# Parameter loads move from ScalarE's queue to SP's, the first scan piece's loads to GpSimd's, and late splits wait for that piece

## The chip, the cores and the metric

The kernel runs on one core of a Trainium2 chip. The core has five engines with an instruction stream each: TensorE (PE: matrix products and transposes into PSUM), VectorE (DVE), ScalarE (ACT), GpSimd (POOL) and SyncE (SP), which here only issues transfers. ScalarE and GpSimd can issue transfers too. An engine takes its instructions in order, so one that waits holds up all behind it. The metric is the device time of one execution in microseconds (us), as the median of several runs.

## The reference

Two layers work on x of shape (8, 64, 64, 96). The first is a selective scan over images (four directions), the second a linear attention and a feed-forward layer with float quantization. The change touches only the first layer:

```python
xz = einsum('bhwc,ec->bhwe', gn(x), in_proj_w); xin, z = split(xz, 2)
xc = silu(depthwise_conv3x3(xin, conv_w) + conv_b)
xs = stack([rows of xc, columns of xc, and both reversed])      # b, K=4, 192, L=4096
dts, Bs, Cs = split(einsum('bkdl,kcd->bkcl', xs, x_proj_weight), [6, 16, 16])
delta = softplus(einsum('bkrl,kdr->bkdl', dts, dt_projs_weight) + dt_bias)
h = h * exp(delta * A) + (delta * u) * Bs                        # 16 states, step by step
y = sum over the states of (h * Cs) + D * u
x = x + out_proj(layer_norm(y) * silu(z))
```

Here `gn` is a group norm over groups of 3 channels; it needs the statistics of a whole image before the first product. The parameters that move are `conv_w`, `conv_b`, the weights of x_proj (`w_xp` in the kernel) and those of the dt projection (`dt_w`).

## The kernel before

Constants are loaded first (`scan_constants`, line 188), then three passes follow. Values that one pass hands to the next go through scratch tensors in DRAM: `u_d` (the convolved x in two orders), `z_d`, `xd_d` (the output of x_proj), `b_d` and `dt_d` (parts of xd_d split into three bfloat16 terms that add up to the float32 value), and `y_d`.

**Pass 1** (line 264) goes over the eight images in pairs. For an image, `statistics` loads eight groups of 512 tokens (tile `xs`), transposes them on TensorE and takes BN statistics on VectorE; `group_norm` turns these into a scale and a bias (`gm`), with two products with `gmat`. `projection` loads the same groups again (`xt`), transposes them, normalises them on ScalarE (`xn`), and multiplies by `w_in` and `w_mix` for x (copied into padded images, `xpad`) and z (to `z_d`). `convolution` runs nine taps of 128 x 4096 on VectorE, then ScalarE's silu into `u`, four transposed copies `ut` and the stores into `u_d`. It comes three times per pair (channels 0 to 127 of either image, and the remaining 64 of both), in the order 0, 2, 1. `x_projection` multiplies by `w_xp` in PSUM tiles `px`, copies them to `xd` (four buffers) and stores these in `xd_d`. A `split` (line 234) loads part of `xd_d` (`bq`), and alternates casts on ScalarE (`bs`) with subtractions on GpSimd, then stores into `b_d` or `dt_d`. For images 0 to 4 the splits run in pass 1; those of images 5 to 7 ("late", since `LATE` is 5), 18 in number, run in pass 2.

**Pass 2** (line 530) goes over 192 pieces of 1024 positions: pair, channel group, direction, part of the image. `prepare` loads `xdt` (6 transfers), `xb` (2) and `u` (1), makes `bT` and `delta` from them with products on TensorE and ScalarE's softplus, then `du` = delta times u on GpSimd. For each of the 16 states ScalarE computes the decay `da`, TensorE the input term in a PSUM tile `wide`, VectorE the scan `h`; `load_c` loads the rows of C broadcast over the partitions (`c`, 1 MB for two states, six buffers), GpSimd multiplies h by c, and TensorE sums over the states. Pass 3 is not touched.

What sets the order: pass 1 and pass 2 are written as generators that `yield` the engine and an estimated cost before each step, or a key that must be done first. `weave` (line 142) runs them by list scheduling when the program is built, and `InOrder` fixes the resulting order on each engine; every operation issued that way has line 91 in the profile. Unless a step is `yield`ed to `weave`, its cost is not in that schedule. In pass 1 and 2 all loads and stores are issued by SP, with two exceptions on ScalarE: the constants of `scan_constants` (`dt_w`, 36 copies from the scratch tensor `w_d`, line 219), and the parameters of pass 1. Of the latter, `later_loads` (line 296) issues `conv_w`, `conv_b` and `w_xp`, 24 transfers, and is called once before `weave` (line 524). So all of these stand ahead of ScalarE's first computation in pass 1. In the built program the transfers of SP and ScalarE signal eight completion counters in turn, and a transfer waits until the one before it on its counter has landed.

Of the kernel before, what the change touches and what calls it, by code (L numbers as in the profile page):

```python
# [42 lines left out]
P = 128  # L43
NB, HH, WW, C = 8, 64, 64, 96
L = HH * WW
DI, N, R, K = 192, 16, 6, 4
# [9 lines left out]
NS = 3  # L56
# [19 lines left out]
def load_by_type(queue, dst, src):  # L76

    queue.dma_start(dst[:, 0], src[0:P])
    queue.dma_start(dst[0:64, 1], src[P:DI])
    queue.dma_start(dst[64:P, 1], src[P:DI])  # L80
# [19 lines left out]
@with_exitstack  # L100
def vss_attn_ffn_kernel(ctx: ExitStack, tc: tile.TileContext, g: dict, out: bass.AP):
    nc = tc.nc
    consts = ctx.enter_context(tc.tile_pool(name="consts", bufs=1))
    dram = ctx.enter_context(tc.tile_pool(name="scratch", bufs=1, space=DRAM))

    ident = consts.tile([P, P], F32, name="ident")
    make_identity(nc, ident)
    mhalf = consts.tile([P, NBLK], F32, name="mhalf")
    nc.vector.memset(mhalf, -0.5)


    u_d = [[dram.tile([DI, L], F32, name=f"u_d{b}_{o}") for o in range(2)] for b in range(NB)]

    y_d = [[dram.tile([L, DI], F32, name=f"y_d{b}_{o}") for o in range(2)] for b in range(NB)]
    z_d = [dram.tile([DI, L], F32, name=f"z_d{b}") for b in range(NB)]
    xd_d = [[dram.tile([2 * NXD, L], F32, name=f"xd_d{b}_{o}") for o in range(2)] for b in range(NB)]

    b_d = [[dram.tile([2, NS, N, L], BF16, name=f"b_d{b}_{o}") for o in range(2)] for b in range(NB)]
    dt_d = [[dram.tile([2, NS, R, L], BF16, name=f"dt_d{b}_{o}") for o in range(2)] for b in range(NB)]

    engines = [InOrder(tc, e) for e in (nc.tensor, nc.vector, nc.scalar, nc.gpsimd)]
    fixed = scan_constants(tc, g, consts, dram, ident)
    pass1(tc, g, consts, ident, mhalf, engines, u_d, z_d, xd_d, b_d, dt_d)
    pass2(tc, g, ident, engines, fixed, u_d, xd_d, b_d, dt_d, y_d)
    pass3(tc, g, ident, mhalf, engines, y_d, z_d, out)

# [61 lines left out]
def scan_constants(tc, g, consts, dram, ident):  # L188

    nc = tc.nc  # L190
    KB = 2 * NS * N
    with tc.tile_pool(name="p0", bufs=1) as tmp:
        a_neg = consts.tile([P, 2, K, N], F32, name="a_neg")
        load_by_type(nc.scalar, a_neg, g["A_logs"].rearrange("(k d) n -> d k n", k=K))
        nc.scalar.activation(a_neg, a_neg, AF.Exp)
        nc.vector.tensor_scalar(a_neg, a_neg, -1.0, None, ALU.mult)
        ds_ = tmp.tile([P, 2, K], F32, name="ds_")
        load_by_type(nc.scalar, ds_, g["DsT"])
        dsum = consts.tile([P, 2], F32, name="dsum")
        nc.vector.tensor_reduce(dsum, ds_, mybir.AxisListType.X, ALU.add)  # L200
        dt_b = consts.tile([P, 2, K], F32, name="dt_b")
        load_by_type(nc.scalar, dt_b, g["dt_biasT"])

        raw = tmp.tile([R, K, DI], F32, name="raw")
        nc.scalar.dma_start(raw, g["dt_wT"])
        by_part = tmp.tile([R, NS, K, DI], BF16, name="by_part")
        for s in range(NS):
            nc.vector.tensor_copy(by_part[:, s], raw)
            if s < NS - 1:
                nc.vector.tensor_sub(raw, raw, by_part[:, s])  # L210
        w_d = dram.tile([R, NS, K, DI], BF16, name="w_d")
        nc.scalar.dma_start(w_d, by_part)
        dt_w = consts.tile([2 * NS * NS * R, 3, K, P], BF16, name="dt_w")
        nc.vector.memset(dt_w, 0.0)
        for c, j, to, ch in ((0, 0, 0, slice(0, P)), (1, 1, 0, slice(0, P)), (2, 0, 0, slice(P, DI)), (2, 1, 64, slice(P, DI))):
            for m in range(NS):
                for s in range(NS):
                    row = ((j * NS + m) * NS + s) * R
                    nc.scalar.dma_start(dt_w[row : row + R, c, :, to : to + ch.stop - ch.start], w_d[:, m, :, ch])

        sel_f = tmp.tile([KB, 2, N], F32, name="sel_f")
        of_part = ident[0:KB, 0:KB].rearrange("p (j s n) -> p j n s", j=2, n=N)
        nc.vector.tensor_reduce(sel_f, of_part, mybir.AxisListType.X, ALU.add)
        sel = consts.tile([KB, 2, N], BF16, name="sel")
        nc.vector.tensor_copy(sel, sel_f)
        sel2 = consts.tile([KB, N, P], BF16, name="sel2")
        for j in range(2):
            nc.vector.tensor_copy(sel2[:, :, 64 * j : 64 * j + 64], sel[:, j, :].unsqueeze(2).to_broadcast([KB, N, 64]))  # L230
    return a_neg, dsum, dt_b, dt_w, sel, sel2


def split(engines, pool_of, cost, src, row, rows, pieces, at, dst):

    act, pool, sp = engines
    wide, used = GRP, rows * pieces
    yield "sp", 0.7, 4.0
    bq = pool_of.tile([P, wide], F32, name="bq")
    src = src[row : row + rows].rearrange("r (s t) -> (r s) t", s=pieces)  # L240
    sp.dma_start(bq[0:used], src[:, at : at + wide])
    yield "act", 0.6
    bs = pool_of.tile([P, NS, wide], BF16, name="bs")
    act.copy(bs[0:used, 0, :], bq[0:used])
    yield "pool", cost
    pool.tensor_sub(bq[0:used], bq[0:used], bs[0:used, 0, :])
    yield "act", 0.6
    act.copy(bs[0:used, 1, :], bq[0:used])
    yield "pool", cost
    pool.tensor_sub(bs[0:used, 2, :], bq[0:used], bs[0:used, 1, :])  # L250
    yield "sp", 0.9
    half = used // 2
    for k2 in range(2):
        to = dst[k2].rearrange("e n (s t) -> (n s) e t", s=pieces)[:, :, at : at + wide]
        sp.dma_start(to, bs[half * k2 : half * (k2 + 1)])
# [5 lines left out]


@with_exitstack
def pass1(ctx, tc, g, consts, ident, mhalf, engines, u_d, z_d, xd_d, b_d, dt_d):
    nc = tc.nc
    pe, dve, act, pool = engines
    sp = InOrder(tc, nc.sync)
# [22 lines left out]
    conv_w = wp.tile([P, 2, 9], F32, name="conv_w")  # L290
    conv_b = wp.tile([P, 2, 1], F32, name="conv_b")

    w_xp = wp.tile([P, 3, 2, P], F32, name="w_xp")
    pool.memset(w_xp, 0.0)

    def later_loads():
        load_by_type(act, conv_w, g["conv_w"])
        load_by_type(act, conv_b, g["conv_b"])
        w0 = 0
        for rows in (slice(R, R + N), slice(R + N, NXD), slice(0, R)):  # L300
            wide = rows.stop - rows.start
            for k2 in range(2):
                src = slice(k2 * NXD + rows.start, k2 * NXD + rows.stop)
                act.dma_start(w_xp[:, 0, :, w0 : w0 + wide], g["x_projT"][0:P, :, src])
                for j in range(2):
                    act.dma_start(w_xp[64 * j : 64 * j + 64, 1 + j, :, w0 : w0 + wide], g["x_projT"][P:DI, :, src])
                w0 += wide


    xpad = [wp.tile([P, HH + 2, WW + 2], F32, name=f"xpad{c}") for c in range(4)]  # L310
# [6 lines left out]
    sts, gms, us, done = {}, {}, {}, {}  # L317
# [112 lines left out]
    def convolution(pair, c):  # L430

        ty = c // 2
        src = xpad[c + pair % 2 if c == 2 else c]
        for b in [2 * pair, 2 * pair + 1] if c == 2 else [2 * pair + c]:
            yield "proj", b
        before = {0: (pair - 1, 1), 2: (pair, 0), 1: (pair, 2)}[c]
        at = 3 * pair + ORDER.index(c) - UB
# [73 lines left out]
    for pair in range(NB // 2):  # L511
# [7 lines left out]
        for b in batches:  # L519
            for o in range(2):  # L520
                units += [("xproj", x_projection(b, o, q)) for q in range(NG)]
                if b < LATE:
                    units += [("split", after(("xd", b, o), split((act, pool, sp), two, 4.4, xd_d[b][o], *w))) for w in splits(b, o, b_d, dt_d)]
    later_loads()
    room = {"proj": 4, "norm": 1, "stats": 3, "xproj": 4, "split": 2, "conv": 3}
    weave([(kind, (list(room).index(kind), i), unit) for i, (kind, unit) in enumerate(units)], room, done)


# [1 line left out]
def pass2(ctx, tc, g, ident, engines, fixed, u_d, xd_d, b_d, dt_d, y_d):  # L530
# [30 lines left out]
    def prepare(at):  # L561
# [9 lines left out]
                yield "split", b  # L571
        yield "sp", 2.5, 3.0
        xdt = one.tile([2 * NS * NS * R, T], BF16, name="xdt")
        for j in range(2):
            for m in range(NS):
                row = (j * NS + m) * NS * R
                sp.dma_start(xdt[row : row + NS * R, :], dt_d[2 * pair + j][o][k2].rearrange("s r t -> (s r) t")[:, cols])
        if at > 0:
            yield "sp", 1.5, 3.0
        xb = two.tile([KB, T], BF16, name="xb")  # L580
        for j in range(2):
            sp.dma_start(xb[j * NS * N : (j + 1) * NS * N, :], b_d[2 * pair + j][o][k2].rearrange("s n t -> (s n) t")[:, cols])
        u = two.tile([P, T], F32, name="u")
        for part, b, ch in parts:
            sp.dma_start(u[part, :], u_d[b][o][ch, cols])

        rows = N * len(parts)
        of_b = sel[:, c, :] if c < 2 else sel.rearrange("p j n -> p (j n)")
# [34 lines left out]

    def late_split(b, o, which):

        yield from split((act, pool, sp), one, 1.25, xd_d[b][o], *which)
        one_more(("split", b), 6, 0.0)

# [508 lines left out]
```

## Time and profile before

| what | time |
|---|---|
| median of three runs | 10281.11 us (10278.86 to 10290.06) |
| the profiled execution | 10274.94 us |
| its span in the trace | 10273.2 us |
| busy: DVE / POOL / ACT / PE | 9587.1 / 9206.3 / 9155.6 / 7658.3 us |
| pass 1, first load to last x_proj output | 0 to 721.4 us |
| first scan of pass 2 | 753.5 us |
| DMA, mean over the span | 205 GB/s |

Busy time excludes register, branch, semaphore and DMA-issuing instructions; the issue of transfers has rows of its own on the timelines, marked SPq, ACTq or POOLq. In a timeline's row the first number is the start, the second the length of a group of instructions; square brackets give the idle time ahead of it and what ended it. PE's clock is granted by a throttle and was 0.895 of full speed on average.

### The profile page before, as it was taken

The numbers are of one execution on the slowest core, as the hardware profiler recorded it, in microseconds if no ns is written. First come the engines' busy times: TensorE is split into PE (matmuls) and PEld (weight loads), VectorE is DVE, ScalarE is ACT, GpSimd is POOL, SyncE is SP. The second block draws the span as 40 slices with busy tenths as digits, with TensorE's granted clock in tenths as the row PEclk, the third lists the DMA queues.
The fourth block names the chain that finished last, engine by engine and source line by source line (L and its number), as shares of the span: only waits on it lengthen the run. The fifth ranks groups of instructions, "written<-read, shape, count | busy, mean of one in ns | idle before, by whom it ended". The sixth has DMA issues, their size and how long they took to land.

```text
span 10273.2 us, 152438 instructions
## 1 busy us (share of the span) xinstructions
PE 7658.3 (75%) x52384; PEld 6303.1 (61%) x52384; DVE 9587.1 (93%) x6886; ACT 9155.6 (89%) x20499; POOL 9206.3 (90%) x3271
## 2 busy tenths in 40 slices
PE   6857777777777777777777777777777777776887
PEld 3326666665666666666666666656666666565675
DVE  6869999999999999999999999999999999997776
ACT  5759999999999999999999999999999999995665
POOL 1539999999999999999999999999999999997886
PEclk8879999989999999989989999999899899997776
DMA  5766676689976676799866666999667668996442
GB/s 148 245 187 219 216 241 219 222 212 206 206 221 215 224 222 215 223 206 201 226 208 222 223 211 223 210 205 212 216 212 231 209 219 220 203 208 172 126 127 58
DMA packets 928007, 2103.28 MB, mean 205 GB/s; under 512 B 274391, under 2 KB 422648, under 8 KB 925700
## 3 DMA queue, kind: packets, MB, share of 16 engines
q1 hardware_dynamic: 919812, 2092.79, 72.1%
q8 instruction: 420, 6.88, 0.3%
q14 instruction: 351, 2.88, 0.1%
q10 hardware_dynamic: 7424, 0.74, 0.1%
HBM read 1917.59 MB, written 175.66 MB: 204 GB/s over the span
## 4 chain that ended last, share of the span: by engine, by line
ACT 29%; DVE 28%; issue 15%; PE 14%; POOL 10%; DMA 4%; SPq 1%; DVEq 0%; ACTq 0%; POOLq 0%
DVE h L91 20%; ACT x L91 11%; ACT da L91 11%; POOL c L91 7%; PE acc L91 6%; DVE wide L91 5%; PE wide L91 3%; ACT L91 2%; PE mm L91 2%; ACT y L91 1%; DVE u L91 1%; ACT delta L91 1%; POOL xg L91 1%; DMA xd_d<-xd 1%; DMA c<-xd_d 1%
## 5 line engine op out<-in xcount | busy, mean ns | idle before, releaser
L91 POOL TENSOR_TENSOR c<-c,h 128x2048 f32<-128x2048 f32 x1536 | 6958.1, 4555 | 293.9 <-issue 143.7
L91 DVE TENSOR_TENSOR_SCAN h<-da,carry,wide 128x1024 f32<-128x1024 f32 x2304 | 5267.5, 2332 | 129.6 <-PE wide L91 31.7
L91 ACT ACTIVATE x<-duT,bT 128x128 f32<-128x128 f32 (+1 forms) x13312 | 3969.7, 368 | 1.9
L91 PE MATMUL acc<-ident,c 128*128 128x128 f32 x24576 | 3424.8, 297 | 583.8 <-POOL c L91 575.4
L91 ACT ACTIVATE da<-delta,a_neg 128x1024 f32<-128x1024 f32 x3072 | 3513.4, 1144 | 309.5 <-DVE h L91 297.3
L91 PEld LDWEIGHTS acc<-ident,c 128*128 128x128 f32 x24576 | 3108.8, 154 | 1019.5 <-POOL c L91 908.8
L91 PE MATMUL wide<-ident,x 128*128 128x128 f32 x10752 | 1557.0, 290 | 654.2 <-DVE h L91 603.7
L91 PEld LDWEIGHTS wide<-ident,x 128*128 128x128 f32 x10752 | 1304.4, 150 | 851.0 <-ACT x L91 393.0
L91 DVE TENSOR_TENSOR_SCAN h<-da,wide 128x1024 f32<-128x1024 f32 x768 | 1713.2, 2271 | 54.1 <-PE wide L91 13.4
L91 DVE TENSOR_TENSOR wide<-du,wide 128x1024 f32<-128x1024 f32 x1280 | 1544.2, 1208 | 56.6 <-PE wide L91 54.9
L91 PE MATMUL wide<-xb,sel 96*128 96x512 bf16 x2560 | 818.8, 403 | 692.6 <-DVE h L91 685.1
L91 POOL TENSOR_TENSOR xg<-duT,bT 128x512 f32<-128x512 f32 (+1 forms) x640 | 893.7, 1412 | 28.4 <-PE wide L91 13.9
L91 PEld LDWEIGHTS <-sel 96*128 96x128 bf16 x2560 | 231.7, 102 | 871.3 <-DVE h L91 623.9
L91 PE MATMUL wide<-ident,xg 128*128 128x128 f32 x3584 | 483.2, 279 | 114.4 <-DVE h L91 112.6
L91 POOL TENSOR_TENSOR du<-delta,u 128x1024 f32<-128x1024 f32 x192 | 457.5, 2383 | 77.8 <-ACT delta L91 77.8
L91 PEld LDWEIGHTS wide<-ident,xg 128*128 128x128 f32 x3584 | 411.5, 144 | 145.3 <-issue 111.7
L91 ACT ACT_TABLE_LOAD x385 | 494.0, 1283 | 6.8
L91 DVE SCALAR_TENSOR_TENSOR u<-xpad,conv_w,u 128x4096 f32<-128x4096 f32 x96 | 458.4, 4775 | 1.9
L91 PE MATMUL px<-u,w_xp 128*128 128x512 f32 x512 | 256.4, 644 | 71.9 <-ACT u L91 45.0
L91 PE MATMUL mm<-w_out,gt 128*128 128x96 f32 (+1 forms) x1024 | 264.4, 378 | 36.5 <-POOL gt L91 16.6
L91 ACT COPY y<-acc 128x1024 f32<-128x1024 f32 x192 | 192.5, 1002 | 87.1 <-PE acc L91 86.7
L91 PEld LDWEIGHTS mm<-w_out,gt 128*128 128x128 f32 (+1 forms) x1024 | 202.0, 243 | 101.0 <-issue 34.6
(133 smaller groups left out, 6219.5 us busy)
## 6 DMA issues: line engine op xcount, KB each, us to landing
c<-xd_d SPq DMA_DIRECT2D x1024, 1024.0 KB
c<-xd_d SPq DMA_DIRECT2D x1024, 512.0 KB
u<-u_d SPq DMA_DIRECT2D x128, 512.0 KB
xdt<-dt_d SPq DMA_DIRECT2D x1152, 36.0 KB
xb<-b_d SPq DMA_DIRECT2D x384, 96.0 KB
u<-u_d SPq DMA_DIRECT2D x128, 256.0 KB
y_d<-y SPq DMA_DIRECT2D x24, 1024.0 KB
y<-y_d SPq DMA_DIRECT2D x64, 384.0 KB
```

What stands on the lines that cost most here:

```text
L91: ins = getattr(self.engine, op)(*args, **kwargs).ins
```

## The change

Four edits. (1) The 36 copies into `dt_w` are no longer issued by `scan_constants`; it returns a function that issues them on a queue given later. (2) `later_loads` becomes a unit of pass 1's schedule and issues on SP: `conv_w` and `conv_b` when the statistics of image 0 are done in the schedule, then `w_xp` in six groups of three, and, when the statistics of image 2 are done, `dt_w`. It declares its costs on SP (3.5, six times 2.0, and 15.0). The convolutions of pair 0 come after the key ("parameters",), which is set when w_xp has been issued. (3) `prepare` of piece 0 issues its nine loads on GpSimd's queue instead of SP's. (4) A late split starts only once all scans of piece 0 are done.

```diff
@@ scan_constants
-        for c, j, to, ch in (...):
-            for m in range(NS):
-                for s in range(NS):
-                    row = ((j * NS + m) * NS + s) * R
-                    nc.scalar.dma_start(dt_w[row : row + R, c, :, to : to + ch.stop - ch.start], w_d[:, m, :, ch])
+        def load_dt_w(queue):
+            for c, j, to, ch in (...):
+                for m in range(NS):
+                    for s in range(NS):
+                        row = ((j * NS + m) * NS + s) * R
+                        queue.dma_start(dt_w[row : row + R, c, :, to : to + ch.stop - ch.start], w_d[:, m, :, ch])
...
-    return a_neg, dsum, dt_b, dt_w, sel, sel2
+    return (a_neg, dsum, dt_b, dt_w, sel, sel2), load_dt_w
@@ pass1
     def later_loads():
-        load_by_type(act, conv_w, g["conv_w"])
-        load_by_type(act, conv_b, g["conv_b"])
+        yield "stats", 0
+        yield "sp", 3.5
+        load_by_type(sp, conv_w, g["conv_w"])
+        load_by_type(sp, conv_b, g["conv_b"])
...
             for k2 in range(2):
+                yield "sp", 2.0
...
-                act.dma_start(w_xp[:, 0, :, w0 : w0 + wide], g["x_projT"][0:P, :, src])
+                sp.dma_start(w_xp[:, 0, :, w0 : w0 + wide], g["x_projT"][0:P, :, src])
...
-                    act.dma_start(w_xp[64 * j : 64 * j + 64, 1 + j, :, w0 : w0 + wide], g["x_projT"][P:DI, :, src])
+                    sp.dma_start(w_xp[64 * j : 64 * j + 64, 1 + j, :, w0 : w0 + wide], g["x_projT"][P:DI, :, src])
...
+        done[("parameters",)] = 0.0
+        yield "stats", 2
+        yield "sp", 15.0
+        load_dt_w(sp)
...
     def convolution(pair, c):
...
+        if pair == 0:
+            yield ("parameters",)
...
-    later_loads()
-    room = {"proj": 4, "norm": 1, "stats": 3, "xproj": 4, "split": 2, "conv": 3}
+    units.append(("later", later_loads()))
+    room = {"later": 1, "proj": 4, "norm": 1, "stats": 3, "xproj": 4, "split": 2, "conv": 3}
@@ pass2, prepare
+        queue = sp if at else pool
...
-                sp.dma_start(xdt[row : row + NS * R, :], ...)
+                queue.dma_start(xdt[row : row + NS * R, :], ...)
...
-            sp.dma_start(xb[j * NS * N : (j + 1) * NS * N, :], ...)
+            queue.dma_start(xb[j * NS * N : (j + 1) * NS * N, :], ...)
...
-            sp.dma_start(u[part, :], u_d[b][o][ch, cols])
+            queue.dma_start(u[part, :], u_d[b][o][ch, cols])
@@ pass2, late_split
+        yield "scans", 0
         yield from split((act, pool, sp), one, 1.25, xd_d[b][o], *which)
```

More of the change, by code (lines that the diff above doesn't have):

```diff
@@ L121, in vss_attn_ffn_kernel @@
     engines = [InOrder(tc, e) for e in (nc.tensor, nc.vector, nc.scalar, nc.gpsimd)]
-    fixed = scan_constants(tc, g, consts, dram, ident)
-    pass1(tc, g, consts, ident, mhalf, engines, u_d, z_d, xd_d, b_d, dt_d)
+    fixed, load_dt_w = scan_constants(tc, g, consts, dram, ident)
+    pass1(tc, g, load_dt_w, ident, mhalf, engines, u_d, z_d, xd_d, b_d, dt_d)
     pass2(tc, g, ident, engines, fixed, u_d, xd_d, b_d, dt_d, y_d)
@@ L214, in scan_constants @@
         nc.vector.memset(dt_w, 0.0)
-        for c, j, to, ch in ((0, 0, 0, slice(0, P)), (1, 1, 0, slice(0, P)), (2, 0, 0, slice(P, DI)), (2, 1, 64, slice(P, DI))):
-            for m in range(NS):
-                for s in range(NS):
-                    row = ((j * NS + m) * NS + s) * R
-                    nc.scalar.dma_start(dt_w[row : row + R, c, :, to : to + ch.stop - ch.start], w_d[:, m, :, ch])
+        def load_dt_w(queue):
+            for c, j, to, ch in ((0, 0, 0, slice(0, P)), (1, 1, 0, slice(0, P)), (2, 0, 0, slice(P, DI)), (2, 1, 64, slice(P, DI))):
+                for m in range(NS):
+                    for s in range(NS):
+                        row = ((j * NS + m) * NS + s) * R
+                        queue.dma_start(dt_w[row : row + R, c, :, to : to + ch.stop - ch.start], w_d[:, m, :, ch])
         sel_f = tmp.tile([KB, 2, N], F32, name="sel_f")
@@ L263, in pass1 @@
 @with_exitstack
-def pass1(ctx, tc, g, consts, ident, mhalf, engines, u_d, z_d, xd_d, b_d, dt_d):
+def pass1(ctx, tc, g, load_dt_w, ident, mhalf, engines, u_d, z_d, xd_d, b_d, dt_d):
     nc = tc.nc
@@ L576, in prepare @@
                 row = (j * NS + m) * NS * R
-                sp.dma_start(xdt[row : row + NS * R, :], dt_d[2 * pair + j][o][k2].rearrange("s r t -> (s r) t")[:, cols])
+                queue.dma_start(xdt[row : row + NS * R, :], dt_d[2 * pair + j][o][k2].rearrange("s r t -> (s r) t")[:, cols])
         if at > 0:
@@ L581, in prepare @@
         for j in range(2):
-            sp.dma_start(xb[j * NS * N : (j + 1) * NS * N, :], b_d[2 * pair + j][o][k2].rearrange("s n t -> (s n) t")[:, cols])
+            queue.dma_start(xb[j * NS * N : (j + 1) * NS * N, :], b_d[2 * pair + j][o][k2].rearrange("s n t -> (s n) t")[:, cols])
         u = two.tile([P, T], F32, name="u")
         for part, b, ch in parts:
-            sp.dma_start(u[part, :], u_d[b][o][ch, cols])
+            queue.dma_start(u[part, :], u_d[b][o][ch, cols])
         rows = N * len(parts)
```

## Prediction

> **What bounds the kernel now.** I read the page first, for the shares and for the row of slices; then busy time by stage, in stretches cut where VectorE's work changes; then each engine's timeline at the two places that the diff touches.
>
> ```profile
> span 10273.2 us, 152438 instructions
> ...
> DVE  6869999999999999999999999999999999997776
> ```
>
> VectorE is full from the fourth slice to the thirty-sixth, which is pass 2 (the scans). The dips are at the ends, and the diff works on the first one. By stage (after the stretch and its length: busy PE, weight loads, DVE, ACT, POOL; clock; DMA share; GB/s):
>
> ```profile
> 0.00:80.00 80.00, 44.89 (x153) 24.45 (x154) 18.67 (x41) 25.09 (x41) 4.66 (x27) 0.79 0.40 99
> 80.00:664.40 584.40, 442.72 (x1220) 209.12 (x1218) 526.75 (x192) 383.01 (x519) 236.28 (x72) 0.86 0.69 209
> 664.40:720.00 55.60, 32.09 (x68) 13.31 (x68) 4.81 (x7) 17.90 (x18) 0.00 (x0) 0.83 0.52 167
> 720.00:753.50 33.50, 4.92 (x22) 2.53 (x22) 3.05 (x3) 5.73 (x7) 3.49 (x2) 0.50 0.76 245
> ```
>
> Before the first convolution tap (80 us), after the last (664.4) and up to the first scan (753.5) VectorE stands nearly still: 142.5 of its 169 us. What shortens these stretches shortens the run, if the stages between only shift.
>
> The start, on ScalarE's timeline and queue (start, length):
>
> ```profile
> 16.97 14.12 ACTq L219 DMA_DIRECT2D dt_w<-w_d  x36
> 31.13 0.34 ACTq L91 DMA_DIRECT2D w_in<-in_in_proj_wT  x1
> ...
> 33.89 1.60 ACTq L91 DMA_DIRECT2D conv_w<-in_conv_w  x3
> 35.87 1.53 ACTq L91 DMA_DIRECT2D conv_b<-in_conv_b  x3
> 37.49 11.77 ACTq L91 DMA_DIRECT2D w_xp<-in_x_projT  x18
> 49.36 1.44 ACT L91 ACTIVATE xn<-pt,gm 96x512 f32<-96x512 f32 x2 [42.37 <-DMA w_xp<-in_x_projT]
> ```
>
> ScalarE issues parameters until 49.26 and only then normalises its first x, though the transposes of that x start at 43.10 and take 1.06. VectorE's first tap follows at 80.10, 13.31 us idle for the projection's copies (xpad).
>
> The boundary between the passes: the last x_proj products; the loads on SP; what they release; then ScalarE and VectorE.
>
> ```profile
> 707.10 4.56 PE L91 MATMUL px<-u,w_xp 128*128 128x512 f32 x10 [1.50 <-DVE xd L91]
> ...
> 722.31 5.72 SPq L91 DMA_DIRECT2D xdt<-dt_d  x6
> 729.38 3.46 SPq L91 DMA_DIRECT2D xb<-b_d  x2
> 732.88 0.42 SPq L91 DMA_DIRECT2D u<-u_d  x1
> ...
> 734.71 0.36 PE L91 MATMUL wide<-sel,xb 96*128 96x16 bf16 x8 [23.06 <-DMA xb<-b_d]
> 736.73 1.11 ACT L91 ACTIVATE delta<-wide,dt_b 128x1024 f32<-128x1024 f32 x1
> 750.40 0.62 ACT L91 CAST bs<-bq 128x512 bf16<-128x512 f32 x1 [12.56 <-DMA bq<-xd_d]
> ...
> 752.33 3.23 ACT L91 ACTIVATE da<-delta,a_neg 128x1024 f32<-128x1024 f32 x3
> 753.51 4.46 DVE L91 TENSOR_TENSOR_SCAN h<-da,wide 128x1024 f32<-128x1024 f32 x2 [7.92 <-ACT da L91]
> ```
>
> Two waits in a row: TensorE waits 23.06 us for xb, and then ScalarE, with delta ready, waits 12.56 us for the load of a late split that is ahead of the decays (da) in its order.
>
> **The change, part by part**
>
> 1. Start. ScalarE's queue loses 36 dt_w issues (14.12) and, behind gmat, 24 more (33.89 to 49.26). In the new order w_in follows w_d at once, 16.97 instead of 31.13: 14.2 earlier. The group mean's product, which waits for gmat (35.32), comes at 21.2, and xs 13 and 14 of SP, which wait for it, at about 24.5. Then SP issues conv_w and conv_b, six loads in 3.5 us by their old row, and the first xt at 28.5. It lands in 2.9 (issued 40.22, used 43.10), plus 1.4 for the transposes: first xn at about 33 instead of 49.4, **16 earlier**. SP then issues three w_xp between one xt and the next, 2.0 by the row (11.77/18 each) and 0.4 for xt: an xt every 2.4 us, faster than ScalarE's 3.3 of work for a group (xn 0.77, four copies or silus of 0.6 and gaps). So ScalarE's 31 us from first xn to first tap stay: first tap at about 64. The convolution's wait for the parameters costs nothing: the last w_xp goes out near 43.
>
> 2. dt_w on SP. 36 copies now stand between the second and third stores of u (ut) and the next xt. At their old 0.39 each they take 14.1, which gives batch 2's projection its 16 back: first xn at about 137, as now (137.52). Covered: batch 2's projection is complete at 178, and the tap that needs it starts at 231 (215 after the shift), so 37 us of slack. Two loads for batch 3's statistics are queued behind too; VectorE reaches them some 32 us after dt_w starts. Past that it stalls one for one. Cost 0.
>
> 3. Splits of batch 4. In the new order of pass 1 two casts stand just ahead of the last silu of u. That silu is late already: the last tap ends at 664.4, the silu starts at 677.8, behind copies that wait for xd_d stores. The casts take the place of one such copy. I take 0, with −8 to +10 as ends: the largest waits of casts there are 10.4 for a load, and a stall of 9.7 for a store could go.
>
> 4. Piece 0's nine loads on GpSimd's queue. On SP they stand behind the last xd_d stores (721.6), and each waits until the transfer eight before it has landed, for SP's and ScalarE's transfers share eight completion counters in the built program. GpSimd is idle since 660 and has counters of its own. There, xdt waits for the last px product (711.7), and xb for the 2 MB store of u issued at 700.5; a younger store had landed by 717.6, so I put xb's issue there. No row shows a transfer issued by GpSimd. The nearest is SP's issue of xdt, 0.33 each. The Trainium skill (DMA: Bandwidth & Descriptors, "Issuing engines are not separate DMA queues") speaks against the move: it saves only the time to initiate. By that rule 9 × 0.33 = 3 us. By the trace the queue stood 722.31 to 733.30 in order and counter waits, and the rule leaves these out. The same page (section "Anatomy of one DMA") gives about 2 us fixed per transfer, which I take as landing time. So I take 1 us an issue: xb and u out by 720, landed by 723.5, first product there instead of 734.71: **11 earlier**. Ends: 13 (the last px copies end at 721.4 and hold the PSUM), and 0 if an issue costs over 2 us.
>
> 5. Late splits held. The 12.56 and the cast's 0.62 go from ScalarE: **13 earlier**. Next late is c: six loads of 1 MB now go out back to back from 718 to 728; at 7.6 to 10.8 us to landing the first is there at about 726, the others 4 us apart, while one pair of scans takes 4.6. First scan at about 729 instead of 753.5. What is held is not removed: each of 18 splits costs GpSimd 2.3 and ScalarE 1.2. The first filled an idle gap; now it runs where both are over 95% busy: **+2**.
>
> 6. Order further on. VectorE's instructions become the same sequence again after an eighth of the list, those of the other engines after at most a quarter: steady state and pass 3 cost 0.
>
> Sum: −16 − 11 − 13 + 2 = **−38**: profiled execution 10274.9 (span 10273.2) to 10237 (span 10235). Three runs had a median of 10281.1, 6 above the profiled one, so the median becomes **10243**.
>
> **Rivals**
>
> A. Pass 1 gives the start back. Its new order is another schedule; VectorE's stalls for xpad (3.5, 13.4, 10.7) are reset by ScalarE and SP, not by the start. For: SP takes 60 issues more, about 28 us. Against: these stalls follow convolutions that do move. Then only the boundary counts: −22, 10259.
>
> B. GpSimd's loads come no earlier (issue over 2 us each, or u's store lands late): −27, 10254. A and B together −11, 10270.
>
> C. The opposite, pass 1 also loses part of its 14.7 us stall for batch 4's statistics (182 to 219), which the new order moves later: −50, 10231.
>
> D. **Slower: dt_w crawls on SP.** With 8 in flight a copy costs an eighth of its landing time. Beside stores that can be large: the last six xd_d took 18 us, 3.0 each. Then 36 take 108, the slack of 37 beyond the planned 14 is exceeded by 57, and the sum is +19: 10300. It decides from 2.5 us a copy on (89 us). Against: at the old place 0.39 with the same counters, and at the new one only two 512 KB stores of u are near.
>
> E. The wait for the first piece has no effect: not so, the new order has no split among the first decays.
>
> **How the numbers follow.** Forecast (−30 to −46) 0.50, C 0.14, B 0.10, A 0.12, A with B 0.08, D 0.06. Something off by 0.2% (20.6 us) is what a measurement can tell: faster than 10260.5 takes the forecast, C, B and most of A, 0.82; slower than 10301.7 half of D and mishaps I do not see, 0.05; within, 0.13. The range 10221 to 10267 takes in C and A, the ends of parts 3 and 4, and leaves out A with B, and D.
>
> **What would show it.** Start: first xn near 33 and first tap near 64; if xn is early and the tap is not, part 1's pacing is wrong. dt_w on SP: 14 us long near 118; much over 50 and D holds. Last tap at 664 − 16; if still at 664, A. Boundary: xb's product 23 us after the last px product now, 12 after; from delta to the first scan 17 us now, 4 after. If TensorE starts pass 2 more than 16 us after its last px product, part 4 is wrong. If GpSimd then waits for DMA c in the first piece, part 5 is.

## The result, and the profile after

| what | before | after |
|---|---|---|
| median | 10282.97 us (10272.16 to 10291.59, 6 runs) | 10234.70 us (10225.52 to 10242.33, 6 runs) |
| ratio, 95% interval | | 0.9953 (0.994 to 0.9966) |
| profiled execution / its span | 10274.94 / 10273.2 us | 10238.11 / 10236.3 us |
| first convolution tap | 80.10 us | 62.19 us |
| last tap ends | 664.38 us | 640.76 us |
| last px product ends | 711.66 us | 690.91 us |
| first scan | 753.51 us | 714.99 us |
| first scan to the end | 9519.7 us | 9521.3 us |

The kernel is 48 us faster by its medians and 37 by the two profiled spans. The page of the profile after:

```profile
span 10236.3 us, 152471 instructions
...
DVE  7969999999999999999999999999999999996776
```

VectorE's row is full over the same slices; its first two digits rose by one. The same four stretches of time as before (stretch and its length, then busy PE, weight loads, DVE, ACT, POOL, clock, DMA share, GB/s):

```profile
0.00:80.00 80.00, 59.47 (x210) 31.91 (x211) 36.44 (x49) 38.44 (x64) 4.66 (x27) 1.00 0.56 144
80.00:664.40 584.40, 435.21 (x1196) 203.43 (x1195) 505.22 (x187) 377.66 (x505) 218.42 (x72) 0.86 0.69 209
664.40:720.00 55.60, 29.20 (x84) 13.31 (x84) 11.40 (x11) 21.61 (x35) 11.55 (x13) 0.75 0.69 221
720.00:753.50 33.50, 23.02 (x170) 20.36 (x169) 31.77 (x17) 32.79 (x74) 31.53 (x9) 0.90 0.62 211
```

VectorE's busy time rose from 18.67 to 36.44 us in the first stretch and from 3.05 to 31.77 in the last: by 753.5 us the scans are running on full engines, where before the first was just starting.

The start, on the timelines of ScalarE and of VectorE (start, length; in brackets the idle time ahead and what ended it):

```profile
16.92 0.34 ACTq L91 DMA_DIRECT2D w_in<-in_in_proj_wT  x1
...
33.28 0.78 ACT L91 ACTIVATE xn<-pt,gm 96x512 f32<-96x512 f32 x1 [26.47 <-DMA w_xp<-in_x_projT]
```

```profile
62.19 2.35 DVE L91 TENSOR_SCALAR u<-xpad,conv_w 128x4096 f32<-128x4096 f32 x1 [9.31 <-ACT xpad L91]
...
409.67 2.35 DVE L91 TENSOR_SCALAR u<-xpad,conv_w 128x4096 f32<-128x4096 f32 x1 [3.00 <-ACT xpad L91]
```

The issue of w_in follows w_d at once, the first xn comes at 33.28 (forecast 33), and the first tap at 62.19 (forecast 64). The second row of VectorE is the second convolution of pair 2; keep its wait of 3.00 us in mind, for it was 13.43 before, and the forecast had no term for it.

The boundary between the passes, all engines:

```profile
691.22 3.28 POOL L91 DMA_DIRECT2D xdt<-dt_d  x6 [35.50 <-PE px L91]
696.48 1.03 POOL L91 DMA_DIRECT2D xb<-b_d  x2 [1.98 <-DMA u_d<-u]
699.09 0.58 POOL L91 DMA_DIRECT2D u<-u_d  x1 [1.57 <-DMA xdt<-dt_d]
702.02 0.69 DVE L91 COPY xd<-px 76x512 f32<-76x512 f32 x1 [3.74 <-DMA xd_d<-xd]
702.86 0.36 PE L91 MATMUL wide<-sel,xb 96*128 96x16 bf16 x8 [11.94 <-DVE xd L91]
...
704.88 1.11 ACT L91 ACTIVATE delta<-wide,dt_b 128x1024 f32<-128x1024 f32 x1
```

TensorE starts pass 2 11.95 us after its last px product (before 23.05). In this execution its wait no longer ends on xb, but on the last copy of px, which frees PSUM. The first scan follows delta by 10.1 us, where the forecast said 4.

### The profile page after: what moved, and what is told of

It reads as the page before. It is cut to its first block, busy times and chain, and to the rows that moved or that the text cites. A ratio compares the mean times of both kernels' runs of the same rounds, so it can differ in the third digit from the quotient of the medians.

```text
span 10236.3 us, 152471 instructions
## 1 busy us (share of the span) xinstructions
PE 7669.6 (75%) x52384; PEld 6320.8 (62%) x52384; DVE 9578.9 (94%) x6886; ACT 9152.3 (89%) x20499; POOL 9194.7 (90%) x3280
## 4 chain that ended last, share of the span: by engine, by line
DVE 28%; ACT 26%; issue 15%; PE 15%; POOL 12%; DMA 3%; SPq 1%; DVEq 0%; ACTq 0%; POOLq 0%
DVE h L91 20%; ACT x L91 10%; ACT da L91 10%; POOL c L91 8%; PE acc L91 6%; DVE wide L91 5%; PE wide L91 3%; ACT L91 2%; PE mm L91 2%; PE px L91 1%; ACT y L91 1%; POOL xg L91 1%; PE pa L91 1%; DMA xd_d<-xd 1%; ACT delta L91 1%
## 5 line engine op out<-in xcount | busy, mean ns | idle before, releaser
L91 POOL TENSOR_TENSOR bq<-bq,bs 128x512 f32<-128x512 f32 (+1 forms) x48 | 121.7, 2536 | 161.4 <-ACT bs L91 140.3
```

The lines of the kernel that those rows point to most:

```text
L91: ins = getattr(self.engine, op)(*args, **kwargs).ins
```

## The experiments

Eleven runs were made, in three groups. Each group was timed beside the kernel before, so times are compared as ratios to it. The places in the traces of all eleven and of the first two profiles are in one table (us; "pass 1" is from the first tap to the end of the last px product, "boundary" from there to the first scan, "rest" from there to the end of the span):

| kernel | first tap | pass 1 | boundary | rest | ratio to before, 95% |
|---|---|---|---|---|---|
| before | 80.1 | 631.6 | 41.9 | 9519.7 | |
| before again (e0) | 79.8 | 637.1 | 40.0 | 9510.5 | |
| GpSimd's queue only (e2) | 80.2 | 640.3 | 38.5 | 9518.4 | 0.9998 (0.999 to 1.0006) |
| hold only (e3) | 80.6 | 634.8 | 35.2 | 9516.7 | 0.9984 (0.9977 to 0.9991) |
| queue and hold (e4) | 80.4 | 645.4 | 23.8 | 9512.1 | 0.9976 (0.9968 to 0.9984) |
| after, no declared cost (e8) | 67.1 | 641.3 | 23.4 | 9511.1 | 0.9974 (0.9964 to 0.9984) |
| start only (e1) | 63.2 | 628.7 | 40.7 | 9515.5 | 0.9974 (0.9965 to 0.9983) |
| after, all parameters on ScalarE (e11) | 77.4 | 626.7 | 25.6 | 9509.0 | 0.9969 (0.9957 to 0.998) |
| after, dt_w on ScalarE (e9) | 75.8 | 623.4 | 24.1 | 9506.8 | 0.9965 (0.9952 to 0.9977) |
| after | 62.2 | 628.7 | 24.1 | 9521.3 | 0.9953 (0.994 to 0.9966) |
| after again (e13) | 62.7 | 627.5 | 22.6 | 9512.1 | 0.9948 (0.9935 to 0.9962) |
| after, six xd buffers (e12) | 62.9 | 619.1 | 25.5 | 9523.6 | 0.995 (0.9937 to 0.9962) |
| after, dt_w eight times (e10) | 63.1 | 718.4 | 22.9 | 9525.3 | 1.0033 (1.0021 to 1.0046) |

In pass 1 the first six rows have the old order of instructions: leaving out the parameter loads, all engines show one and the same sequence in these six traces up to the last tap. e1, e11, e13, e12 and e10 show exactly the sequence of the changed kernel. e9, which also drops dt_w's declared cost, has an order of its own, and a nearer one to the old: of 233 instructions of VectorE, 6 stand more than two places from where they stood before, against 65 in the changed kernel. "New order" below means an order with declared costs, e9's included where it is named.

**e1, the start alone.** Edits 1 and 2; `queue = sp` for every piece and no `yield "scans", 0` in the late splits.

> The kernel before with the parameters' loads and dt_w on SP only (edits 1 and 2); piece 0's loads stay on SP and no late split is held. Theory (the parts add up; the start gives 16 to 18 and pass 1 keeps it and gains a little): last x_proj product about 691 instead of 711.7, first scan about 733 instead of 753.5, time -18 to -21 us. Rival A (pass 1 gives the start back): first tap early, last tap at 664, time 0. Rival C (pass 1 gains a lot more): last tap before 635, time -29.

The median fell from 10277.19 to 10251.72. First tap at 63.16, last tap ends 640.78, last px product at 691.82 and first scan at 732.49: the places are those of the theory, with the last tap 23 to 30 us ahead of the 663.9 to 670.6 of the kernels with the old start and the old order. The median gained 25 us (interval 17 to 36) where 18 to 21 were expected; e0 below says why more. By time alone rival C's 29 stays possible, but its last tap before 635 did not come.

**e2, GpSimd's queue alone.**

```diff
+        queue = sp if at else pool
-                sp.dma_start(xdt[row : row + NS * R, :], ...)
+                queue.dma_start(xdt[row : row + NS * R, :], ...)
-            sp.dma_start(xb[j * NS * N : (j + 1) * NS * N, :], ...)
+            queue.dma_start(xb[j * NS * N : (j + 1) * NS * N, :], ...)
-            sp.dma_start(u[part, :], u_d[b][o][ch, cols])
+            queue.dma_start(u[part, :], u_d[b][o][ch, cols])
```

> The kernel before with piece 0's nine loads on GpSimd's queue only (edit 3). Theory: the first product of pass 2 comes 12 us after the last px product instead of 23; the late split's load, queued behind those nine on SP, comes as much earlier, so the first scan comes 11 earlier and the time is -11 us. Rival 1 (the load of the late split lands at 750 anyway): first product 11 earlier, first scan unchanged, time 0. Rival 2 (only the time to initiate is saved): -3 us.

Its timeline at the boundary, where the last px product ends at 720.51:

```profile
731.99 0.36 PE L91 MATMUL wide<-sel,xb 96*128 96x16 bf16 x8 [11.49 <-DMA xb<-b_d]
734.01 1.11 ACT L91 ACTIVATE delta<-wide,dt_b 128x1024 f32<-128x1024 f32 x1
...
755.85 0.62 ACT L91 CAST bs<-bq 128x512 bf16<-128x512 f32 x1 [20.72 <-DMA bq<-xd_d]
```

The first product comes 11.5 us after px, as in the changed kernel, and little is gained by it: ScalarE's wait for the late split grew from 12.56 to 20.72. Counted from the last px product, the cast comes at 35.3, and at 38.7 and 36.9 in the two profiles of the kernel before. The time is unchanged within 0.1%. That excludes the theory's 11 us, but not the 3 of rival 2. What speaks against rival 2 is the first product, which came some 10 us earlier and not 3. Rival 1 is the nearer: the split's load came only 2 to 3 us earlier. What an earlier product saves is spent in the next wait.

**e3, the hold alone.**

```diff
     def late_split(b, o, which):
+        yield "scans", 0
```

> The kernel before with the late splits held only (edit 4). Theory of the prediction: first product of pass 2 stays at 734.7, first scan 4 us after delta, at about 741: time -13 + 2 = -11 us. Rival, from the profile of the changed kernel, where the first scan came 10 us after delta behind du and its products: if u is what was late there, 741; if the chain delta, du, transposes, products takes 10 us by itself, first scan at about 747, time -5 us.

```profile
741.82 1.11 ACT L91 ACTIVATE delta<-wide,dt_b 128x1024 f32<-128x1024 f32 x1
743.01 2.35 POOL L91 TENSOR_TENSOR du<-delta,u 128x1024 f32<-128x1024 f32 x1 [78.09 <-ACT delta L91]
...
745.42 1.97 PE L91 MATMUL wide<-ident,du 128*128 128x128 f32 x8 [4.38 <-POOL du L91]
748.33 2.36 DVE L91 TENSOR_TENSOR wide<-du,wide 128x1024 f32<-128x1024 f32 x2 [22.29 <-PE wide L91]
750.60 8.81 DVE L91 TENSOR_TENSOR_SCAN h<-da,wide 128x1024 f32<-128x1024 f32 x4
```

Here u had been issued at 737.94 by SP and was no cause of delay: GpSimd waits for delta alone. Still the scan starts 8.8 us after delta. Row by row these are: softplus 1.1, du 2.35, the transposes of du 1.97, the products behind them on TensorE, and VectorE's products of du with them, 2.36. So the chain takes this by itself, as the rival said; the decays (744.25) are no longer what is late. The boundary shortened by 4.8 to 6.7 us against the three kernels with neither edit, near the rival's 5. The time fell by more, from 10277.19 to 10262.44: its interval (9 to 24 us) leaves 5 out and has the theory's 11 in it, though the scan did not come 4 us after delta. Where the remainder came from, the one profile does not show.

**e4, both.** Edits of e2 and e3 together.

> The kernel before with edits 3 and 4 (GpSimd's queue and the hold), without the start. Theory of the prediction (-11 -13 +2): first scan at about 729, time -22 us. What the profile of the changed kernel suggests (first scan 24 us after the last px product, since u lands late on GpSimd's queue): first scan at about 736, time -18 + 2 = -16 us.

The boundary is 23.8 us, the second value of the two expectations (24), and the first scan comes 8.8 us after delta; u, issued by GpSimd at 734.87, was there in time. The time of the scan (749.57) met neither, because pass 1 ended late in this execution. The run took 10254.55 against 10277.19: 22.6 less, interval 16 to 33, which is the first value (22) and does not quite exclude the second (16). So by the traces the queue is worth 35.2 − 23.8 = 11.4 us with the hold, and 1.5 to 3.4 without it; the hold is worth 38.5 − 23.8 = 14.7 with the queue, and 4.8 to 6.7 without it. Each of the two waits hid most of the other's removal.

**e0, the kernel before again.**

> The kernel before, profiled once more. In the kernels of the last comparisons that keep its pass 1, the last px product ended at 711.7, 720.5, 715.4 and 725.8 us, though pass 1 has the same instructions. If that is the spread of executions, it ends anywhere from 708 to 726 here, and the distance from it to the first scan stays 42. If it belongs to the edits at the boundary, it ends at 711.7 within 2 us.

The last px product ended at 716.89, with the boundary at 40.0. Five executions of the same pass 1 have thus given 711.7, 715.4, 716.9, 720.5 and 725.8, and that of the first profile is the lowest. Its pass 1 was 631.6 us long, where the six with the old order have a mean of 638.4.

**e8, the new loads in the old order.** In `later_loads` all three declared costs on SP become 0, which leaves the scheduler's picture as it was:

```diff
-        yield "sp", 3.5
+        yield "sp", 0.0
...
-                yield "sp", 2.0
+                yield "sp", 0.0
...
-        yield "sp", 15.0
+        yield "sp", 0.0
```

> The changed kernel, but later_loads declares no cost on SP, so the schedule gives pass 1 the order of the kernel before, with the parameters' loads still on SP. First tap at 62 to 64 in both theories. Theory (the start brings 16 to 18, and the 6 to 8 us that pass 1 gains on top come from its new order): last tap ends at 649 (the mean of four kernels with the old order, 666.7, less 17.6), time -40 us against the kernel before. Rival (the early start brings all of it): last tap ends at 641, time -48 us as the changed kernel.

VectorE's wait ahead of the second convolution of pair 2:

```profile
430.89 2.35 DVE L91 TENSOR_SCALAR u<-xpad,conv_w 128x4096 f32<-128x4096 f32 x1 [18.23 <-ACT xpad L91]
```

The first xn came at 33.2, but the first tap only at 67.1 (3 to 5 later than expected), and the last tap at 661.0, later than both values. The time fell by 24 us (interval 16 to 37), which misses both values too: 40 and 48. Pass 1 took 641.3 us, a time of the old order. Of the 13 us of its earlier first tap, only 6.5 were left at the last tap (667.5 is the mean of the five kernels that start late with this order). The wait above took 18.2 us. VectorE's waits for transposes of statistics add up to 31 us in this pass 1, and to 22 to 25 in those five; that is about what was lost.

**e11, the new order with the old start.** All parameters and dt_w issued by ScalarE at their old places; the declared costs stay, as steps that issue nothing.

> The changed kernel's order in pass 1 (its declared costs stay), with all parameters and dt_w issued by ScalarE at the old places; GpSimd's queue and the hold stay. First tap at 80. Theory (the new order alone gives 6 to 8 us of pass 1): last tap ends at about 659 instead of 667, time 17 us more than the changed kernel. Rival (the order gives nothing): last tap ends at 667, time 25 us more than the changed kernel.

First tap at 77.4, last tap at 656.0 (theory 659, rival 667), pass 1 626.7 us. The ratio 0.9969 is 16 to 22 us above the two values of the changed kernel, where the theory said 17; its interval, 12 wide to either side, would not tell 17 from the rival's 25, so it is the places that decide. Pass 1 is as short as with the early start, and the first tap itself came 2.8 us earlier by the order alone. The wait ahead of the same convolution, here in the second profile of the kernel before and then in this kernel:

```profile
435.63 2.35 DVE L91 TENSOR_SCALAR u<-xpad,conv_w 128x4096 f32<-128x4096 f32 x1 [20.33 <-ACT xpad L91]
```

```profile
423.94 2.35 DVE L91 TENSOR_SCALAR u<-xpad,conv_w 128x4096 f32<-128x4096 f32 x1 [5.49 <-DMA z_d<-z]
```

It is 13.4, 20.3, 17.2, 15.2, 17.8 and 18.2 us in the six traces with the old order, and 3.0, 2.4, 6.2, 5.5, 7.5 and 2.9 in six with a new one (after, e1, e9, e11, e13, e12). That is 12.4 in the mean, about as much as the difference of pass 1, 638.4 − 627.0 (without e12, which differs in another way) = 11.4. Without e9 the difference is 10.5.

The traces also show what came sooner. First the kernel before, then the changed one: the first tap of the convolution ahead (pair 2's first), before also a copy of px that still waits for a store of xd_d, and ScalarE's first copy of image 5 into xpad.

```profile
376.85 2.34 DVE L91 TENSOR_SCALAR u<-xpad,conv_w 128x4096 f32<-128x4096 f32 x1
378.14 0.58 ACT L91 COPY xd<-px 76x512 f32<-76x512 f32 x1 [2.64 <-DMA xd_d<-xd]
386.79 0.58 ACT L91 COPY xpad<-pa 128x512 f32<-128x512 f32 x1
```

```profile
363.31 2.34 DVE L91 TENSOR_SCALAR u<-xpad,conv_w 128x4096 f32<-128x4096 f32 x1
367.54 0.59 ACT L91 COPY xpad<-pa 128x512 f32<-128x512 f32 x1
```

In the six traces with the old order that copy into xpad comes 9.9 to 13.4 us after the tap, and image 5's copies take 45.5 to 49.2 us from first to last; in the six with a new one it is 3.5 to 7.6 and 41.5 to 43.4. So ScalarE is less far behind VectorE there. e9 shows that this does not need the whole new order.

**e9, dt_w back on ScalarE.**

```diff
 def scan_constants
+        load_dt_w(nc.scalar)
 def later_loads
-        yield "stats", 2
-        yield "sp", 15.0
-        load_dt_w(sp)
```

> The changed kernel with the 36 copies into dt_w back on ScalarE ahead of w_in; conv_w, conv_b and w_xp stay on SP. Theory (the start is set by ScalarE's queue ahead of gmat, where dt_w takes 14.1 us; the rest of the start's gain, about 3, is the parameters behind it): first xn at about 47, first tap at about 76, time 14 us more than the changed kernel. Rival (the parameters behind gmat are what held xn, dt_w was beside it): first xn at about 35, time as the changed kernel.

First xn at 46.7, first tap at 75.8: the theory, within 0.3. Of the 17.5 us of the start 13 are dt_w. Of the other 4.4, the first xn shows 2.7 (49.4 to 46.7), which are the parameters behind gmat; the rest lies between xn and the tap, where e11 gained 2.7 by the order alone. The ratio is 12 to 17 us above the changed kernel's two; its own interval is 13 wide to either side, so time alone would not have told it from the rival.

**e13, the changed kernel again.**

> The changed kernel once more, beside the kernel before. If pass 1 of the old order ends later by 11.5 us from the first tap to the last px product (mean 638.4 in six kernels, 626.9 in four of the new order), that distance is 624 to 630 here, the last px product ends at 686 to 693, and the time is 44 to 48 us below the kernel before. Rival (the profiled pair is right, 37): distance 632 or more, -37 us.

10226.66 against 10278.96: 52 us, interval 39 to 67. Pass 1 took 627.5, and the last px product ended at 690.2. The first profiles' 37 was too little, mostly because the kernel before had been profiled in a favourable execution: it lay 8 us below its median, and the changed kernel's 3 above.

**e10, dt_w eight times.**

```diff
-        load_dt_w(sp)
+        for again in range(8):
+            load_dt_w(sp)
```

> The changed kernel with the 36 copies into dt_w issued eight times in a row at their place on SP: 252 copies more, 89 us at 0.355 each. Theory with the slack that the prediction gave (37 us, and one for one beyond it): +52 us against the changed kernel. With the slack read off the changed kernel's trace (image 2's projection complete at 179.1, its first tap at 200.5: 21 us): +68 us. Rival (nothing waits for what stands behind dt_w within 89 us): 0. Rival (a copy there takes 2.5 us or more once many are in flight): +600 us or more.

SP's queue, and VectorE:

```profile
113.85 100.45 SPq L91 DMA_DIRECT2D dt_w<-w_d  x288
214.34 2.21 SPq L91 DMA_DIRECT2D xt<-in_x  x4
216.65 0.99 SPq L91 DMA_DIRECT2D xs<-in_x  x2
```

```profile
228.09 0.69 DVE L91 BATCH_NORM_STATS2 st<-pt 96x6 f32<-96x512 f32 x1 [79.05 <-PE pt L91]
```

A copy takes 0.349 us with 288 in line, and 0.355 with 36 in the changed kernel, so they do not crawl at this place. But the 87.7 us that are added cost 88.5 (10315.2 against 10226.66, each with an interval of 13 to either side), more than the theories that counted slack (52 and 68). VectorE stalls 79.05 us. It does so not at the tap of image 2, but at the statistics of image 3, whose two loads (xs) stand last behind dt_w. It wanted them at 149.0, and they were ready 13.8 us after the last copy's end. So dt_w could take 149.0 − 113.85 − 13.8 = 21 us; the 36 copies take 12.8, which leaves 9.

**e12, six xd buffers.**

```diff
+    xd_p = ctx.enter_context(tc.tile_pool(name="p1xd", bufs=6))
-        xd = four.tile([2 * NXD, GRP], F32, name="xd")
+        xd = xd_p.tile([2 * NXD, GRP], F32, name="xd")
```

> The changed kernel with six xd buffers in a pool of their own instead of four: ScalarE's and VectorE's copies of the x_proj output waited 34 and 38 us for the stores of xd_d in the tail of pass 1. Theory (the tail from the last silu to the last px product, 42.7 us, is held by these buffers; in the old order it takes 33): tail 34 to 38, time -5 to -9 us against the changed kernel. Rival (the tail is held by the stores themselves, or by TensorE): tail 42 to 43, time 0.

The waits between 640 and 705 us, in total, with their number and the longest, first in e13, then here:

```profile
DVE xd L91 <- DMA xd_d<-xd: 35.9, 6, 11.1
```

```profile
DVE xd L91 <- DMA xd_d<-xd: 18.2, 3, 9.4
```

The buffers did hold the tail: the last px product ends at 682.0, 35.0 us after the start of the last silu, against 690.2 and 44.8 in e13. But TensorE then waited 14.7 us instead of 11.3. The last px copy had ended at 692.2, so what it waited for must be xb (the trace names nothing), which GpSimd issued at 689.13, behind its wait for the store of u. The first scan came at 707.5, 5.4 earlier than in e13, and the time is the same (10228.2 and 10226.66, both with intervals of about 13). A gain of 5 us is neither shown nor excluded; no version of these is clearly faster than the changed kernel.

## Why the prediction was right

The forecast had the mechanism of the start and both waits at the boundary. Its sum is near also because two terms that it had wrong nearly cancel, which is luck.

The median of 10234.7 lies 8 below the forecast of 10243 and within its range. By the means of the table the sum is −17.5 (first tap: 80.2 to 62.7, three kernels with all of the start's edits) −11.4 (pass 1) −16.9 (boundary: 40.8 in three kernels, 23.9 in six) = −46; the two comparisons measured 48 and 52. The forecast was −38. Term by term:

- **Part 1, the start: −16, measured −17.5.** First xn at 33 held, and e9 gives dt_w the share that the part gave it. Moving the loads is worth 13.1 in the old order (e8) and 14.7 in the new (e11's 77.4 to 62.7); the other 2.8 are the order's, which the part did not count. ScalarE's 31 us from first xn to first tap stayed within 3: they were 28 to 29 in the new order and 34 in e8.
- **Part 2, dt_w on SP: cost 0, right, but with the wrong cover.** Named as slack were 37 us to image 2's tap. In the changed kernel that has 21 (tap at 200.5, not 215; its projection complete at 179.1). What decides is the statistics of image 3: the part had VectorE reach them 32 us after dt_w starts (35 in e10), but did not take off the 13.8 us from the last copy to their transposes. That leaves 9 us beyond dt_w's 13; a dt_w of twice the length would not fit. Rival D was excluded by e10: 0.349 a copy, not 2.5.
- **Part 3, the tail: 0, right only as a sum.** From the last tap to the last px product it took 46 to 57 us in the old order and 48 to 51 in the new (e10 and e12 left out). The last silu starts earlier after its tap (4 to 9 us instead of 13 to 22), and the products then take 9 longer in the mean, held by the xd buffers, as e12 shows. The part had named a stall that could go, but not the longer products.
- **Part 4, GpSimd's queue: −11, measured −11.4**, with the hold in place. Its steps were off and made up for each other. An issue cost 0.55 us, not 1, and xb went out 3.6 to 7.1 us after the last px product. Landing took longer than the 2 us that the part took from the page: in six of nine traces with this edit the product came 6.5 to 7.7 us after the last issue of xb and 1.0 to 4.5 after the last px copy, and e2's row names xb as what it waited for. In the other three, the changed kernel's first profile among them (702.86), it came 0.15 after that copy: there PSUM set the time, which the part had named as its upper end. The rule of the Trainium skill (DMA: Bandwidth & Descriptors, "Issuing engines are not separate DMA queues") that only the time to initiate is saved gave −3. It leaves out what stood ahead of these loads in SP's stream: before, six stores of xd_d had taken 18.0 us there. How much of the other 8 us is this order and how much the shared counters, no run separates.
- **Part 5, the hold: −13 of wait, right, but not −13 of scan.** The row of 12.56 went. The part's sign of being wrong did appear: GpSimd waited for c once, 4.3 us from 709.7 on; but this is beside the chain to the first scan. What is late next was mis-sized: 4 us from delta to the first scan, measured 8.8 in e3 and e4, 10.1 in the changed kernel, where u landed 1.3 late. In the trace of before, du (GpSimd), its transposes and VectorE's products lay under the wait for bq, and the part costed only ScalarE's side, delta to da. So parts 4 and 5 together gave 17 instead of 24. The +2 for the held work is too small to be seen: the rest is 9510 to 9520 in the four kernels without the hold, and 9507 to 9521 in the seven with it (e12 and e10 left out).
- **The order of pass 1: 0 in the sum, measured −11.4.** This is the term that failed. Rival A argued that stalls follow convolutions that move, and in the old order it is half true: e8 lost 6.5 of 13 us of its start. Rival C had the size, −12, but named the wait for the statistics of image 4. Such waits did not shrink (VectorE's waits for transposes of statistics are 23 us in pass 1 before and 29 after). What shrank is the wait for the copies into xpad ahead of the second convolution of pair 2, a row that the forecast had read (13.4) and had used only as a risk. Two errors of opposite sign, −11 here and +7 at the boundary, left the sum 8 off.

That the order is the cause is shown by e8 and e11: each has the instruction sequence of one kernel with the parameter loads of the other, and its pass 1 takes as long as in the kernel whose sequence it has. The traces show ScalarE less far behind; which of the moved steps does this was not tried. Not tried either was making du on an engine other than GpSimd.

## What to carry to other kernels

When a wait is removed, walk every engine's chain from the released value to the next operation of the engine that bounds, not only the chain that was waiting: work that ran under the old wait becomes the new one, and two edits at one boundary may each be worth little alone (here 1.5 to 3.4 and 4.8 to 6.7 us of the boundary, 17 together). When the scheduler is told of moved work, its new order is an edit of its own; it can be measured alone, with the costs declared and the work left in place. And when a queue gets more to do, look for the load standing last behind it, with its earliest reader; that sets the cover.

## What was not expected of the hardware

With the same sequence of instructions, parameter loads apart, pass 1 took 631.6 to 645.4 us in six traces. The spread is 0.13% of the whole, and it lies in the stalls for xpad and for statistics and in the tail. So a single pair of profiles was 11 to 15 us off the medians of many runs. GpSimd's issue of a transfer of 18 x 1024 or 128 x 1024 took 0.55 to 0.58 us; SP's took 0.42 for the same u.
